# Turning the expert items' rows with a DMA transpose of two 16-bit planes

## The chip, the cores and the metric

The kernel runs on one core of one Trainium2 chip. The metric is the device time of one execution in microseconds. A core has engines that each run their own instruction stream: TensorE (PE, matrix multiply; its weight loads are listed as PEld), VectorE (DVE), ScalarE (ACT), GpSimd (POOL) and SyncE (SP). Sixteen DMA engines move data; SP, ACT and POOL issue transfers to them. SBUF is the working memory of 128 partitions, PSUM holds what TensorE writes, DRAM holds the inputs and outputs. Engines wait for one another by semaphores.

## The reference

One transformer block with adaptive layer norm, in float32, for 2 sequences of 2048 tokens and 256 features (4096 tokens in all). Six modulation vectors come from a small conditioning input.

```python
h = _layernorm(x) * (1 + ca) + sa
x = x + ga * attention(h)            # causal, 2 heads of 128, one shared k and v, rotary
h = _layernorm(x) * (1 + cb) + sb
x = x + gb * ffn(h)

# ffn: 8 experts, 256 -> 1024 -> 256, gated per token
gate = softmax(h @ Wg + bg)
thr = sigmoid(h @ Wt + bt) * 0.125
w = where(gate >= thr, gate - thr, 0); w = w / sum(w)
out = sum over e of w[e] * (gelu(h @ W1[e] + b1[e]) @ W2[e] + b2[e])
```

A token is worked on only by the experts whose weight is above zero.

## The kernel before

**Attention stage.** Work goes by tiles of 128 tokens, the two sequences in turn. For each tile the kernel loads x, normalizes it, projects q, k and v, applies the rotation, computes scores against all earlier keys in chunks of 512, takes the softmax, multiplies with v, projects, adds the residual, stores it to the output, normalizes again into `hx` (the features that the experts read), stores `hx` to the DRAM tensor `feats`, and computes the gate's logits. The order of all these steps on all engines is worked out at build time by a planner (`Plan`): each step has an engine, an assumed cost, the steps it comes after, and buffers that it takes and gives back; the planner simulates the engines and emits the steps in the order in which they would start. A changed cost can therefore change the order of every engine. The step `n_f` in `tile_steps` is the store of `hx` (issued by SP), and the step that copies the transposed `hx` for the gate comes after it. Small per-row statistics (`rstd`) are computed on POOL. At the end of each group of tiles the kernel writes the entries of expert 0's token list by indirect DMAs from POOL.

**Expert stage** (`experts`). For each expert there is a list of its tokens. The work is cut into items of up to 256 tokens (`TI`), that is two blocks of 128 (`CI`); the last item of an expert may have one block. The number of items is known only at run time, so every engine has its own loop over experts and items and they are tied together by semaphores that count up. The items are numbered through by `t`. For one item:

- POOL copies the item's token numbers into `at` (L1060) and gathers the tokens' rows of `feats` into `xr` by one indirect DMA for each block (L1018, semaphore "loaded"). `xr` is a single buffer, so POOL first waits until the previous item's rows are turned ("turned"). In the first items of each expert it also writes four pieces of the next expert's list (L1039). Then it adds an earlier item's result to the output by two indirect DMAs (L1049).
- TensorE turns the rows: features must lie on the partitions for the first product. `turn(t + 1)` (L888) makes four 128 x 128 transposes of `xr` into the PSUM tile `pT`; it stands just before the last of the eight first products of item t.
- VectorE copies `pT` to `xT` in SBUF (L963, semaphore "ready"), after the last first product of item t has read the old `xT`. `xT` is a single buffer too. After that it adds the bias to the item's result (`yb`, L986), and then waits until the earlier scatter has landed, multiplies with the gate and leaves the result in `yo`.
- TensorE multiplies with the first weights (L910, into `h`) and, two steps behind, with the second weights (L899, into `y`). In the trace a float32 matmul of one 128 x 128 weight block is two records. ScalarE applies the Gelu between the two (L937).
- SP reads each expert's list from DRAM into a sheet (L877) as soon as its last entry is written. ScalarE's queue loads the weights of experts 2 to 7.

The code touched by the change, and what calls it:

Of the kernel before, what the change touches and what calls it, by code (L numbers as in the profile page):

```python
# [11 lines left out]
F32 = mybir.dt.float32  # L12
BF16 = mybir.dt.bfloat16
I32 = mybir.dt.int32
ET = mybir.EngineType
# [4 lines left out]
P = 128  # L20
B, T, D = 2, 2048, 256
HS, NH = 128, 2
E, FF = 8, 1024
KD = D // P
# [73 lines left out]
def adaln_block_kernel(ctx, tc, x, wqkvT, woT, wgt, bgt, w1, b1T, w2, b2, cT, wmod, rope, out):  # L98
# [15 lines left out]

    nc = tc.nc
# [17 lines left out]
    feats = dram.tile([NTOK, D], F32, name="feats")  # L133
# [11 lines left out]
    for e in range(RES, E):  # L145
# [3 lines left out]
    xr = ep.tile([P, CI, D], F32, name="xr")  # L149
# [14 lines left out]
    pT = pp.tile([P, KD, TI], F32, name="pT")  # L164
    experts(
        tc, nc, lists, feats, out.rearrange("b t d -> (b t) d"), counts, ident, b1_sb, b2_bc,
        gb_bc, w1, w2, weights, xr, xT, gs, gate, part, yb, yo, sheets, at, mcur, who, to, new, place,
        entry, hs, ys, pT,
# [3 lines left out]
def attention(  # L172
# [7 lines left out]
    room = {"ps": 6, "pav": 2, "x": 9, "s": 18, "pT": 3, "hx": 4, "qT": 3, "big": 3, "xn": 3,  # L180
# [213 lines left out]
    def tile_steps(b, i, r, group, g):  # L394
# [239 lines left out]
        def hx():  # L634
# [9 lines left out]
        n_f = add(  # L644
            "SP", 0.8, lambda: nc.sync.dma_start(feats[ts(b * NT + i, P), :], st["hx"]), [n_h],
            late=2.0,
# [172 lines left out]
def experts(  # L819
    tc, nc, lists, feats, rows, counts, ident, b1_sb, b2_bc, gb_bc, w1, w2, weights, xr, xT, gs,  # L820
    gate, part, yb, yo, sheets, at, mcur, who, to, new, place, entry, hs, ys, pT,
# [40 lines left out]
    with tc.tile_critical():  # L862
        names = (
            "read", "loaded", "turned", "ready", "first", "act", "second", "taken", "parted",
            "gated", "copied", "named", "biased", "added", "waited", "indexed", "staged",
# [4 lines left out]
        with nc.Block() as block:  # L870

            @block.sync
            def _(sync):
                for e in range(E):
# [5 lines left out]

            @block.tensor
            def _(pe):
                def turn(t):

                    pe.wait_ge(sem["loaded"], t * (16 * CI) + 16 * CI)
                    for c in range(CI):
                        for k in range(KD):
                            last = pe.transpose(pT[:, k, ts(c, P)], xr[:, c, ts(k, P)], ident)  # L888
                    last.then_inc(sem["turned"], 1)

                def item(e, i, t, parts):
# [13 lines left out]
                    pe.wait_ge(sem["ready"], t + 1)  # L905
                    for f in range(NF):
                        if f == NF - 1:
                            turn(t + 1)
# [17 lines left out]
                turn(0)  # L926
# [3 lines left out]
            def _(act):  # L930
# [11 lines left out]
                def begin(e):  # L942

                    if e == 0:

                        act.wait_ge(sem["turned"], 1)
# [13 lines left out]
            def _(dve):  # L960
                def ready(t):
                    dve.wait_ge(sem["turned"], t + 1)
                    dve.tensor_copy(xT, pT).then_inc(sem["ready"], 1)  # L963
# [209 lines left out]
```

## Time and profile before

The table gives the timed runs and one profiled execution, which has a time of its own.

| what | value |
|---|---|
| runs before | median 1737.94 us of 3 (1736.16 to 1740.65) |
| the profiled execution's own time | 1731.92 us |
| its span, first to last instruction | 1729.6 us |
| mean granted TensorE clock in the span | 0.985 of full speed |
| TensorE busy | 1667.1 us, 96% of the span |
| VectorE, ScalarE, POOL busy | 669.1, 685.4, 841.4 us |
| DMA traffic | 83.61 MB, 48 GB/s over the span |

How to read it: the page cuts the span into 40 equal slices of about 43 us and gives each engine's busy share in tenths; PEclk is the granted TensorE clock in tenths. The expert stage begins about 506 us after the start. The chain that ended last follows the work back from the last instruction, each time to what released it. A timeline line gives the start and the length in microseconds, the engine, the line of the kernel, the operation, the tile written and the tiles read, the shape, and in brackets how long the engine had stood idle and who ended that. Lines of DMA issues end with the size of one and the median time from issue to landing. An engine's busy time can overlap with itself, above all TensorE's.

### The profile page before, as it was taken

Reading aid. Unit: us, or ns where it says so; the run is one execution under the profiler, and the core shown is the slowest. Engines: PE = TensorE matmul, PEld = TensorE weight load, DVE = VectorE, ACT = ScalarE, POOL = GpSimd, SP = SyncE. Lnnn points to the kernel's source line nnn. Section 1 sums busy time; section 2 is a strip of 40 time slices with the busy share of each in tenths; the row PEclk is TensorE's granted clock in tenths of the full one; section 3 lists DMA queues with packets and bytes.
Section 4 is the critical chain, followed back from the end, with each engine's and each line's share of the span. In section 5 each row is a group of like instructions: output and inputs, shape, how many; then the busy total and the mean of one; then the engine's idle time right before and its main releaser. Section 6 shows DMA issues by size and latency. Waiting matters only on the chain.

```text
span 1729.6 us, 26689 instructions
## 1 busy us (share of the span) xinstructions
PE 1667.1 (96%) x8021; PEld 1386.7 (80%) x8021; DVE 669.1 (39%) x2126; ACT 685.4 (40%) x1475; POOL 841.4 (49%) x968
## 2 busy tenths in 40 slices
PE   6899999999959999999999999999999999999996
PEld 4576666767748888888888888888888888888886
DVE  5887757566522223322222322222232222222322
ACT  1455555555513334333333333333333333333332
POOL 2331122020037757765775774666577467644433
PEclk9999999999979999999999999999999999999998
DMA  5311000000022223223223222322322222222222
GB/s 196 113 32 34 29 28 29 16 16 16 13 75 37 37 44 89 40 41 83 40 42 82 47 37 44 80 38 43 83 42 42 36 38 38 44 36 36 46 37 34
DMA packets 72489, 83.61 MB, mean 48 GB/s; under 512 B 16944, under 2 KB 63792, under 8 KB 72304
## 3 DMA queue, kind: packets, MB, share of 16 engines
q0 software_dynamic: 42784, 47.50, 17.1%
q1 hardware_dynamic: 21776, 22.86, 4.0%
q10 hardware_dynamic: 7872, 12.58, 2.2%
q8 instruction: 25, 0.41, 0.1%
q14 instruction: 32, 0.26, 0.1%
HBM read 50.38 MB, written 32.51 MB: 48 GB/s over the span
## 4 chain that ended last, share of the span: by engine, by line
PE 92%; DVE 4%; DMA 1%; issue 1%; POOL 1%; ACT 1%; POOLq 0%; SPq 0%; DVEq 0%; ACTq 0%
PE h L910 34%; PE y L899 34%; PE pav L580 7%; PE psc L498 6%; PE ptr L570 3%; PE pq L442 3%; PE pT L888 2%; PE po L614 1%; DMA list<-entry,place 1%; PE pl L661 1%; PE pr L482 1%; DVE s L509 0%; DVE x L621 0%; PE ph L652 0%; DVE hx L639 0%
## 5 line engine op out<-in xcount | busy, mean ns | idle before, releaser
L910 PE MATMUL h<-xT,w 128*128 128x256 f32 (+1 forms) x2816 | 673.5, 372 | 0.8 <-DVE xT L963 0.8
L899 PE MATMUL y<-w,g 128*128 128x256 f32 x2704 | 669.9, 379 | 0.0
L937 ACT ACTIVATE g<-h,b_sb 128x256 f32<-128x256 f32 (+1 forms) x704 | 327.6, 466 | 755.4 <-PE h L910 754.1
L910 PEld LDWEIGHTS h<-xT,w 128*128 128x128 f32 x2816 | 518.2, 191 | 67.6 <-issue 1.5
L899 PEld LDWEIGHTS y<-w,g 128*128 128x128 f32 x2704 | 510.6, 190 | 67.7
L1049 POOL DMA_INDIRECT out<-yo,who x180 | 294.6, 1636 | 119.8 <-DVE yo L998 71.8
L963 DVE COPY xT<-pT 128x512 f32<-128x512 f32 x89 | 61.6, 692 | 619.8 <-PE h L910 609.0
L1039 POOL DMA_INDIRECT list<-new,to x228 | 234.0, 1026 | 99.1 <-issue 50.3
L1018 POOL DMA_INDIRECT xr<-feats,at x178 | 179.8, 1010 | 108.2 <-POOL at L1060 74.7
L498 PE MATMUL psc<-kT,qT 128*128 128x512 f32 (+3 forms) x320 | 145.9, 542 | 1.6 <-ACT qT L487 1.1
L580 PE MATMUL pav<-pT,v 128*128 128x256 f32 x544 | 143.6, 386 | 0.8 <-ACT pT L574 0.7
L937 ACT ACT_TABLE_LOAD x88 | 112.9, 1283 | 29.1 <-issue 16.9
L525 ACT ACTIVATE s<-s,nmx 128x512 f32<-128x512 f32 (+3 forms) x160 | 104.1, 653 | 50.0 <-DVE nmx L516 49.9
L986 DVE TENSOR_TENSOR yb<-y,b_bc 128x256 f32<-128x256 f32 x169 | 64.2, 420 | 150.3 <-PE y L899 150.3
L509 DVE TENSOR_SCALAR_CACHE_REDUCE s<-psc 128x512 f32<-128x512 f32 (+3 forms) x160 | 95.4, 606 | 65.0 <-PE psc L498 44.0
L1060 POOL COPY at<-sheet 128x2 int32 (+1 forms) x88 | 44.7, 508 | 150.1 <-PE pT L888 145.9
L580 PEld LDWEIGHTS pav<-pT,v 128*128 128x128 f32 x544 | 94.8, 190 | 25.9 <-issue 14.2
L766 POOL DMA_INDIRECT list<-entry,place x32 | 34.2, 1069 | 129.4 <-DVE place L763 78.5
L574 ACT COPY pT<-ptr 128x512 f32<-128x512 f32 (+1 forms) x144 | 76.8, 563 | 47.2 <-PE pav L580 23.1
L388 POOL TENSOR_SCALAR rstdf<-mvf 128x1 f32<-128x1 f32 x32 | 9.3, 291 | 164.2 <-DVE mvf L384 68.1
L570 PEld LDWEIGHTS ptr<-ident,s 128*128 128x128 f32 x544 | 65.6, 145 | 16.4 <-ACT s L525 5.0
L977 DVE SCALAR_TENSOR_TENSOR gate<-gb_bc,mcur,part 128x256 f32<-128x256 f32 x176 | 77.5, 482 | 3.1
(133 smaller groups left out, 1145.5 us busy)
## 6 DMA issues: line engine op xcount, KB each, us to landing
w<-in_w ACTq DMA_DIRECT2D x12, 1024.0 KB, 7.4
x<-in_x SPq DMA_DIRECT2D x32, 128.0 KB, 2.1
out<-x SPq DMA_DIRECT2D x32, 128.0 KB, 1.7
feats<-hx SPq DMA_DIRECT2D x32, 128.0 KB, 1.8
w<-in_w SPq DMA_DIRECT2D x4, 1024.0 KB, 10.2
list<-new,to POOLq DMA_INDIRECT x228
out<-yo,who POOLq DMA_INDIRECT x180, 3.9
xr<-feats,at POOLq DMA_INDIRECT x178
```

What stands on the lines that cost most here:

```text
L498: nc.tensor.matmul(ps[:, :w], st["qT"][:, h, :], kT[:, ds(c * SC, w)], start=True, stop=not last)
L509: nc.vector.tensor_scalar(s[:, :w], st["sc", h, c][:, :w], 1.0, None, ALU.mult, ALU.max, accum_out=st["mx", h][:, c : c + 1],)
L525: nc.scalar.activation(s[:, :w], s[:, :w], AF.Exp, bias=st["nmx", h], accum_out=st["den"][:, h, c : c + 1],)
L570: nc.tensor.transpose(ptr[:, j, h, :], s[:, ds((c0 + j) * P % SC, P)], ident)
L580: nc.tensor.matmul(st["pav"][:, : NH * P], v[:, c0 + j, :], st["pT", c0][:, j].rearrange("p h t -> p (h t)"), start=(c0 + j == 0), stop=(c ...
L899: last = pe.matmul(ys[c], gs[f % 4][:, ts(c, P)], weights[e][1][:, f, :], start=(f == 0), stop=(f == NF - 1),)
L910: last = pe.matmul(hs[f % 4][:, :w], weights[e][0][:, k, ts(f, P)], xT[:, k, :w], start=(k == 0), stop=(k == KD - 1),)
L937: act.activation(gs[f % 4][:, :w], hs[f % 4][:, :w], AF.Gelu_apprx_tanh, bias=b1_sb[:, at : at + 1],).then_inc(sem["act"], 1)
L977: last = dve.scalar_tensor_tensor(gate[:, c, :], gb_bc[:, 1, :], mcur[:, c, 1:2], part[:, c, :], ALU.mult, ALU.add,)
L1018: pool.indirect_dma_start(out=xr[:, c, :], out_offset=None, in_=feats, in_offset=bass.IndirectOffsetOnAxis(ap=at[:, c : c + 1], axis=0),). ...
L1039: pool.indirect_dma_start(out=lists[e], out_offset=bass.IndirectOffsetOnAxis(ap=to[:, j : j + 1], axis=0), in_=new[:, j, :], in_offset=Non ...
L1049: pool.indirect_dma_start(out=rows, out_offset=bass.IndirectOffsetOnAxis(ap=who[:, c : c + 1], axis=0), in_=yo[:, c, :], in_offset=None, b ...
```

## The change

In the attention stage POOL now splits the 32-bit features of a tile into a plane of the low 16-bit halves and a plane of the high halves (`hp`), and SP stores these planes: each row of `feats` has 256 low halves and then 256 high halves, as many bytes as before. The copy for the gate now comes after the split, where it came after the store. In the expert stage the gather brings the same bytes into `xr`, seen as 16-bit elements. SP then issues one DMA transpose of `xr` (128 rows by 1024 halves) into a new SBUF tile `xp` (eight blocks of 128 x 128 halves), when the rows are loaded and VectorE has emptied `xp`; its semaphore is "planed". VectorE joins the halves of `xp` into 32-bit words of `xT` with one copy for each block. TensorE's turn, the PSUM tile `pT` and the semaphore "turned" are gone. POOL, ScalarE and VectorE wait for "planed" where they waited for "turned". SP runs a loop over experts and items of its own, and its read of the next expert's list stands in that loop after the items that write the list.

```diff
-    feats = dram.tile([NTOK, D], F32, name="feats")
+    feats = dram.tile([NTOK, 2 * D], U16, name="feats")
...
-    xr = ep.tile([P, CI, D], F32, name="xr")
+    xr = ep.tile([P, CI * 2 * D], U16, name="xr")
+    xp = ep.tile([P, CI * 2 * KD, P], U16, name="xp")
...
-        n_f = add(
-            "SP", 0.8, lambda: nc.sync.dma_start(feats[ts(b * NT + i, P), :], st["hx"]), [n_h],
-            late=2.0,
+        def halves():
+            st["hp"] = work([P, 2, D], "hp", u, U16)
+            nc.gpsimd.tensor_copy(
+                st["hp"], st["hx"].bitcast(U16).rearrange("p (d two) -> p two d", two=2)
+            )
+
+        n_f = add("POOL", 1.2, halves, [n_h], take=["hp"])
+        add(
+            "SP", 0.8,
+            lambda: nc.sync.dma_start(
+                feats[ts(b * NT + i, P), :], st["hp"].rearrange("p two d -> p (two d)")
+            ), [n_f], late=2.0, give=["hp"],
         )
...
             @block.sync
             def _(sync):
-                for e in range(E):
+                def read(e):
                     if e > 0:
                         sync.wait_ge(sem["written"], (e * NP + 1) * (16 * NW))
                     sync.dma_start(
                         sheets[e], lists[e].rearrange("(p c) f -> p c f", p=P)
                     ).then_inc(sem["read"], 16)
+                def turn(t):
+                    sync.wait_ge(sem["loaded"], t * (16 * CI) + 16 * CI)
+                    sync.sem_inc(sem["paused"], 1)
+                    sync.wait_ge(sem["ready"], t + 1)
+                    sync.sem_inc(sem["paused"], 1)
+                    sync.dma_start_transpose(xp, xr).then_inc(sem["planed"], 16)
+
+                read(0)
+                turn(0)
+                done, t0 = 1, 0
+                for e in range(E):
+                    many = items_of(sync, count(sync, e, NTOK))
+                    if e == E - 1:
+                        run(sync, many, NTOK // TI, lambda i: turn(t0 + i))
+                    else:
+                        a = count(sync, E + e, NP)
+                        run(sync, a, NP, lambda i: turn(t0 + done + i))
+                        read(e + 1)
...
+                turn(t0)
             @block.tensor
             def _(pe):
-                def turn(t):
-                    pe.wait_ge(sem["loaded"], t * (16 * CI) + 16 * CI)
-                    for c in range(CI):
-                        for k in range(KD):
-                            last = pe.transpose(pT[:, k, ts(c, P)], xr[:, c, ts(k, P)], ident)
-                    last.then_inc(sem["turned"], 1)
-
...
-                    pe.wait_ge(sem["ready"], t + 1)
+                    pe.wait_ge(sem["ready"], t + 2)
                     for f in range(NF):
-                        if f == NF - 1:
-                            turn(t + 1)
...
-                        act.wait_ge(sem["turned"], 1)
+                        act.wait_ge(sem["planed"], 16)
...
                 def ready(t):
-                    dve.wait_ge(sem["turned"], t + 1)
-                    dve.tensor_copy(xT, pT).then_inc(sem["ready"], 1)
+                    dve.wait_ge(sem["planed"], t * 16 + 16)
+                    dst = xT.bitcast(U16).rearrange(
+                        "p k (c t two) -> p c k t two", c=CI, two=2
+                    )
+                    src = xp.rearrange("p (c two k) t -> p c k t two", c=CI, two=2)
+                    for c in range(CI):
+                        last = dve.tensor_copy(dst[:, c], src[:, c])
+                    last.then_inc(sem["ready"], 1)
...
+                dve.sem_inc(sem["ready"], 1)
                 ready(0)
...
                 def item(e, i, t, also=None):
-                    wait("turned", t)
+                    wait("planed", t * 16)
...
-                wait("turned", 1)
+                wait("planed", 16)
                 scatter(0)
```

## The prediction

> **What bounds the kernel now.** I read the page's slices first, then the chain that ended last, then the timeline of one item.
>
> ```profile
> PE   6899999999959999999999999999999999999996
> PEclk9999999999979999999999999999999999999998
> PE 92%; DVE 4%; DMA 1%; issue 1%; POOL 1%; ACT 1%; POOLq 0%; SPq 0%; DVEq 0%; ACTq 0%
> ```
>
> TensorE is full from slice 12 on (from about 506 us, the expert stage) at nearly full clock, and 92% of the chain that ended last lies on it. A busy PE may overlap its own matmuls, so I go by starts. One item in the middle of the expert stage (timeline, start and length in us):
>
> ```profile
> 1003.85 1.03 PE L899 MATMUL y<-w,g 128*128 128x256 f32 x4
> ...
> 1010.76 1.03 PE L899 MATMUL y<-w,g 128*128 128x256 f32 x4
> 1011.62 0.60 PE L888 MATMUL pT<-ident,xr 128*128 128x128 f32 x4
> 1012.06 1.03 PE L910 MATMUL h<-xT,w 128*128 128x256 f32 x4
> 1012.92 2.75 PE L899 MATMUL y<-w,g 128*128 128x256 f32 x12
> 1013.21 0.69 DVE L963 COPY xT<-pT 128x512 f32<-128x512 f32 x1 [7.39 <-PE h L910]
> 1015.51 2.75 PE L910 MATMUL h<-xT,w 128*128 128x256 f32 x12
> ```
>
> A group of four matmul records takes (1010.76 - 1003.85) / 8 = 0.864 us; an item of two blocks has 16 groups, 13.82 us. The four turns take 1012.06 - 1011.62 = 0.44 from start to start, although the page gives each 273 ns (they overlap). Copies into xT stand 14.25 us apart: 13.82 + 0.43. There is no gap: TensorE sets the item, and the copy (done 1013.90, needed 1015.51) is hidden. The spacing of the 89 copies shows 88 items and one last idle turn; 7 items have one block (7.56 us).
>
> The next engine in line is POOL. Its own item where it also writes a list:
>
> ```profile
> 1013.80 0.76 POOL L1060 COPY at<-sheet 128x2 int32 x1
> 1015.41 1.02 POOL L1018 DMA_INDIRECT xr<-feats,at  x1 [0.85 <-POOL at L1060]
> ...
> 1024.27 1.61 POOL L1049 DMA_INDIRECT out<-yo,who  x1 [0.30 <-issue]
> 1026.18 1.60 POOL L1049 DMA_INDIRECT out<-yo,who  x1 [0.30 <-issue]
> 1027.19 0.80 POOL L1060 COPY at<-sheet 128x2 int32 x1
> ```
>
> From copy to copy 13.39 us with no wait for PE. In the other items (about 32) it waits up to 4.8 us for the turn, so needs about 9.4 us there. POOL is slower than nobody, but 13.4 stands close under 13.82.
>
> **The change, part by part.**
>
> *The turns leave TensorE.* Every one of the 88 items holds one turn of 0.43 us: 88 x 0.43 = -37.8 us. The chain's own share for L888, 2% of 1730 us, agrees. Nothing else was late at these points, so the next item simply starts earlier.
>
> *The DMA transpose, T, and where it lies.* SP waits until xr is loaded and the last join has emptied xp, then turns 128 x 1024 halves (256 KB) in one DMA. The join of item t ends about 1 us before item t starts, so the transpose for item t+1 starts then and is needed 13.8 - 1.2 us later: xp alone hides T up to about 11 us. Tighter is xr, also single: gather, transpose, gather. The gather's part is read at the start of the stage:
>
> ```profile
> 498.96 0.18 POOL L1060 COPY at<-sheet 128x2 int32<-128x2 int32 x1 [4.13 <-DMA sheet<-list]
> ...
> 504.08 1.12 PE L888 MATMUL pT<-ident,xr 128*128 128x128 f32 x4 [12.68 <-DMA xr<-feats,at]
> 505.24 0.69 DVE L963 COPY xT<-pT 128x512 f32<-128x512 f32 x1 [10.82 <-PE pT L888]
> 505.98 5.06 PE L910 MATMUL h<-xT,w 128*128 128x256 f32 x12 [0.78 <-DVE xT L963]
> ```
>
> From the index copy to landed data 5.1 us. The loop 5.1 + T must stay under 13.82: T up to 8.7 us costs nothing. No transpose stands in the trace. Lower end: a plain DMA.
>
> ```profile
> w<-in_w ACTq DMA_DIRECT2D x12, 1024.0 KB, 7.4
> feats<-hx SPq DMA_DIRECT2D x32, 128.0 KB, 1.8
> ```
>
> Along these two (5.6 us for 896 KB), 256 KB lands in 2.6 us. [...] so I take 3.5 us, near the rows[...]. The 16 DMA engines are 20 to 30% busy in this stage, room for 256 KB more an item. With T = 3.5 the cover is 5 us.
>
> *The join.* One copy of 0.69 us from PSUM becomes two of 512 halves each from SBUF. The nearest row is the copy sc_bc<-sc of 512 elements inside SBUF, 0.42 us; the other end is the 0.69 of now. Two make 0.84 to 1.38, with the gap about 0.9 to 1.5. The window is 1013.21 to 1015.51, 2.3 us: hidden in a whole item. In an item of one block only six records of y follow, 6 x 0.216 = 1.3 us from 1714.49, the copy began 1714.78, so 1.0 us is left: a stall of 0 to 0.5 us in 7 items, taken as +1.5 us in all. The wait for the transpose stands ahead of yb on VectorE, which PE waits for as "taken" in the next item: a late T would hit both at once.
>
> *Start of the stage, once.* From landed data to the first matmul it took 505.98 - 504.08 = 1.9 us (four turns, copy). Now T 3.5 + join 1.2 + two handovers 0.2 = 4.9: +3.0 us[...].
>
> *Waits that change owner.* POOL's gather waits for "planed" where it waited for "turned"; since the transpose runs at the start of the item before, not at its end, POOL is freed earlier and its 4.8 us waits shrink: nothing gained, it was hidden. ScalarE waits for the first transpose before it asks for expert 2's weights: 3 us later, needed twenty items on; the first Gelu behind it comes after the first matmul anyway. POOL's first scatter starts about 3 us later too; it stood at item 1's index at 512.45, over 8 us ahead of item 1. On SP the read of the next list now stands behind the transposes of the items that write it. Who waits for it are POOL and VectorE at the next expert's start; two or more items without list writes (POOL's 4.8 us waits come in runs of two or more) lie between, 27 us for a read that lands in 1.8. All these: 0.
>
> *Attention stage.* 32 times POOL splits hx into halves (512 elements) and SP stores after it. POOL's copy of 256 words took 0.63 us, the memset of 1024 took 0.94: 0.6 to 1.3 us each, 20 to 40 us in all on an engine that is 11 to 26% busy in these 500 us. The store comes about 1.3 us later; hx is held till both readers are done; the last store (486.81) then ends about 490, and the first gather is at 499.99. Behind the split on POOL stand the rstd steps, which VectorE needs. From 100 to 400 us PE is 97 to 100% busy and covers that; in the first and last 100 us (79 and 83 busy) a delay can show. The planner's costs change, so the order of the steps changes on every engine, with the same matmuls. I take 0, with -8 to +10.
>
> Sum: -37.8 + 3.0 + 1.5 = -33.3. Against the profiled execution's own 1731.92 (span 1729.6 and 2.3 around it) this is 1698.6; the runs' median 1737.94 lies 6 above it, and 1737.94 - 33.3 gives 1704.6. I say 1704.
>
> **Rivals.**
>
> A. *The transpose is the new bound* (slower). [...] It decides from 88 x (5.1 + T) = 1210, T = 8.65 us. [...] Against it: the plain rows, 3 times under that point. Chance 0.06.
>
> B. *The attention stage pays.* POOL's splits delay rstd where PE has no queue, or the new order is worse: 1.3 us on some ten tiles, +13: about 1717. For it: PE's idle time in the first and last 100 us. Against: the middle is full. Chance 0.12.
>
> C. *The join becomes a new wait.* If reading two planes alternately costs over 1.3 us a copy, the pair outlasts the 2.3 us window and each item stalls; at 1.35 us it takes back the 0.43: about 1738, no change. Against it: the 0.42 row. Chance 0.05.
>
> D. *POOL becomes the bound.* Its 13.4 us is 0.4 under the new item. [...] Chance 0.05.
>
> **Numbers.** Likeliest 0.72, at 1704, its own range 1694 to 1714. About 0.3% (5 us) is what a measurement can tell. Faster: 0.72 + B 0.12 + D 0.05 = 0.89; same: C 0.04 of its 0.05, rounded; slower: A and a rest of C, 0.07. The range leaves out A, C and the far ends: 1691 to 1720.
>
> **What the profile would show.** Right: no L888 row, matmul groups 0.864 us apart across the item's end, joins 13.82 us apart, a transpose landing in 3 to 4 us, the stage near 1175 us. Wrong: VectorE's join waiting on the transpose DMA in each item (A), PE waiting on the join (C), the join or PE waiting on gathers (D), the first expert matmul more than 10 us later than 506 (B).

## The result and the profile after

| | before | changed | difference |
|---|---|---|---|
| timed runs, median | 1737.7 us (1736.16 to 1740.65, 4 runs) | 1720.95 us (1719.86 to 1721.61, 4 runs) | ratio 0.990, 95% interval 0.988 to 0.992 |
| profiled execution | 1731.92 us | 1719.86 us | -12.1 |
| its span | 1729.6 us | 1718.0 us | -11.6 |
| granted TensorE clock | 0.985 | 0.982 | |

The change is faster by 1.0%. That is the sign that was forecast and about half of the size (1704 us, 1691 to 1720), and the time lies 1 us outside the range. The ledger of the two profiled executions, in the terms of the prediction's sum:

| part of the span | before | changed | difference | predicted |
|---|---|---|---|---|
| start to the first index copy (attention stage) | 498.96 | 504.48 | +5.5 | 0 |
| index copy to the first expert matmul | 7.02 | 9.69 | +2.7 | +3.0 |
| first to last expert matmul | 1209.97 | 1189.42 | -20.6 | -36.3 |
| last matmul to the end | 13.65 | 14.41 | +0.8 | 0 |

Two rows are off: 5.5 us in the attention stage, and 15.7 us in the expert stage. TensorE's slices, the chain that ended last and the groups of the changed kernel, from its page (busy us, mean ns, then the idle time before and who ended it):

```profile
PE   6999999999949999999999999999999999999996
PEclk9999999999979999999999999999999999999998
PE 89%; DVE 5%; DMA 2%; issue 1%; POOL 1%; ACT 1%; POOLq 0%; SPq 0%; DVEq 0%; ACTq 0%
L944 PE MATMUL h<-xT,w 128*128 128x256 f32 (+1 forms) x2816 | 675.1, 373 | 17.5 <-DVE xT L1001 17.4
L935 PE MATMUL y<-w,g 128*128 128x256 f32 x2704 | 673.5, 380 | 10.8 <-ACT g L970 8.6
L970 ACT ACTIVATE g<-h,b_sb 128x256 f32<-128x256 f32 (+1 forms) x704 | 326.3, 466 | 736.0 <-PE h L944 663.8
L1089 POOL DMA_INDIRECT out<-yo,who x180 | 295.1, 1639 | 239.1 <-DVE yo L1037 186.4
L1001 DVE COPY xT<-xp 128x512 uint16<-128x512 uint16 x178 | 72.3, 448 | 686.8 <-PE h L944 601.0
```

The row of the turns is gone, the clock is nearly the same (0.982 against 0.985, and the groups keep their 0.864 us), and TensorE still holds the chain. The first products' 17.4 us behind the join are the one wait at the start of the stage. The new thing is in the second products (L935): 10.8 us of idle time, mostly behind ScalarE's Gelu. The same row before, with POOL's scatter and index copy:

```profile
L899 PE MATMUL y<-w,g 128*128 128x256 f32 x2704 | 669.9, 379 | 0.0
L1049 POOL DMA_INDIRECT out<-yo,who x180 | 294.6, 1636 | 119.8 <-DVE yo L998 71.8
L1060 POOL COPY at<-sheet 128x2 int32 x87 | 44.6, 512 | 145.9 <-PE pT L888 145.9
```

POOL's 145.9 us of waiting for the turn are gone; it now waits 186.4 us for `yo`, at the scatter. In the order of POOL's program that is behind the gather and the list writes, so these run earlier than they did.

A two-block item in the middle of the stage went as forecast (timeline of the changed kernel):

```profile
1000.26 1.03 PE L944 MATMUL h<-xT,w 128*128 128x256 f32 x4
1001.12 2.75 PE L935 MATMUL y<-w,g 128*128 128x256 f32 x12
1001.42 0.77 DVE L1001 COPY xT<-xp 128x512 uint16<-128x512 uint16 x2 [7.72 <-issue]
1003.71 2.75 PE L944 MATMUL h<-xT,w 128*128 128x256 f32 x12
1006.30 1.03 PE L935 MATMUL y<-w,g 128*128 128x256 f32 x4
```

From the last group of first products (1000.26) to the next item's (1003.71) are 3.45 us, four groups of 0.864, with nothing between them. The two copies of the join take 0.77 us, and 1.5 us are left between their end (1002.19) and the next item. Starts of two-block items stand 13.81 us apart, where it was 14.25.

So the loss is elsewhere. Here is each one-block item by the start of its first matmul to that of the next item's:

| one-block item | 1 | 2 | 3 | 4 | 5 | 6 | sum |
|---|---|---|---|---|---|---|---|
| before | 7.47 | 7.47 | 7.54 | 7.47 | 7.60 | 7.59 | 45.1 |
| changed | 9.13 | 9.84 | 11.73 | 12.08 | 7.95 | 7.04 | 57.8 |

(The seventh ends the program.) With 0.43 us less each they should come to 42.5: the six lose 15.3 us, and three two-block items (14.26, 14.63, 15.15) another 2.6. The first of the six, with ScalarE and POOL:

```profile
655.11 1.50 PE L944 MATMUL h<-xT,w 128*128 128x128 f32 x12
656.22 0.96 POOL L1079 DMA_INDIRECT list<-new,to  x1 [0.30 <-issue]
656.71 0.37 ACT L970 ACTIVATE g<-h,b_sb 128x128 f32<-128x128 f32 x1 [2.22 <-PE h L944]
657.21 0.69 PE L935 MATMUL y<-w,g 128*128 128x256 f32 x2 [0.60 <-issue]
657.74 0.61 PE L944 MATMUL h<-xT,w 128*128 128x128 f32 x4
657.91 1.61 POOL L1089 DMA_INDIRECT out<-yo,who  x1 [0.73 <-issue]
658.90 0.37 ACT L970 ACTIVATE g<-h,b_sb 128x128 f32<-128x128 f32 x1 [1.82 <-PE h L944]
659.32 0.70 PE L935 MATMUL y<-w,g 128*128 128x256 f32 x2 [0.97 <-ACT g L970]
```

The same place before:

```profile
650.81 1.50 PE L910 MATMUL h<-xT,w 128*128 128x128 f32 x12
651.46 1.26 ACT L937 ACTIVATE g<-h,b_sb 128x128 f32<-128x128 f32 x3 [1.26 <-PE h L910]
652.15 0.60 PE L899 MATMUL y<-w,g 128*128 128x256 f32 x2
652.58 0.61 PE L910 MATMUL h<-xT,w 128*128 128x128 f32 x4
```

Before, ScalarE began 0.65 us after the item's first matmul (651.46 - 650.81); here it began 1.60 us after (656.71 - 655.11), and the three groups of first products were all finished by then. TensorE ran them at the usual pace and then stood at the second product, whose input is that Gelu. The record of TensorE's signal stands 24 ns ahead of ScalarE's start, so ScalarE was not slow: the signal came late.

I call it a late start when a Gelu begins more than 0.2 us after both its first product (by the record's end) and ScalarE's earlier work, its table load included, were done. The profiled execution of before has none; that of the changed kernel has 84, 82.7 us in all. (The expectations below count 89 with 84 us there, and 4 with 2.2 us in before. Those counts leave the table load out: the 4 of before, and 5 of the 89, are first Gelus of an item for which ScalarE was still loading its table.) In a two-block item TensorE's first products are two groups of 0.86 us ahead of the second products, and most of the late starts are hidden: 65 of them, 62.9 us in all, go with the 2.6 us that these items lose. In a one-block item the two groups are 0.43 us each, and most is paid: 19 late starts, 19.8 us in all, go with the 15.3 us.

The start of the stage answers the estimate of the transpose:

```profile
504.48 0.18 POOL L1100 COPY at<-sheet 128x2 int32<-128x2 int32 x1 [4.32 <-DMA sheet<-list]
...
509.77 1.33 SPq L901 DMA_TRANSPOSE xp<-xr  x1
...
513.30 0.82 DVE L1001 COPY xT<-xp 128x512 uint16<-128x512 uint16 x2 [13.57 <-DMA xp<-xr]
...
514.17 2.07 PE L944 MATMUL h<-xT,w 128*128 128x256 f32 x4 [17.43 <-DVE xT L1001]
```

From the issue to the join are 3.53 us (T was taken as 3.5), and from the index copy to the issue 5.3 (gather, taken as 5.1).

### The profile page after: what moved, and what is told of

It reads as the page before. It is cut to its first block, busy times and chain, and to the rows that moved or that the text cites. A ratio compares the mean times of both kernels' runs of the same rounds, so it can differ in the third digit from the quotient of the medians.

```text
span 1718.0 us, 26912 instructions
## 1 busy us (share of the span) xinstructions
PE 1635.1 (95%) x7665; PEld 1355.1 (79%) x7665; DVE 678.2 (39%) x2215; ACT 684.3 (40%) x1475; POOL 863.9 (50%) x1000
## 3 DMA queue, kind: packets, MB, share of 16 engines
q0 software_dynamic: 42784, 47.50, 17.4%
q1 hardware_dynamic: 115760, 46.21, 11.6%
## 4 chain that ended last, share of the span: by engine, by line
PE 89%; DVE 5%; DMA 2%; issue 1%; POOL 1%; ACT 1%; POOLq 0%; SPq 0%; DVEq 0%; ACTq 0%
PE h L944 34%; PE y L935 34%; PE pav L584 6%; PE psc L502 5%; PE pq L446 3%; PE ptr L574 3%; DMA list<-entry,place 1%; PE po L618 1%; DVE s L513 1%; PE pl L674 1%; PE pr L486 1%; PE ph L665 0%; DVE hx L643 0%; DVE x L625 0%; DVE t L462 0%
## 5 line engine op out<-in xcount | busy, mean ns | idle before, releaser
L944 PE MATMUL h<-xT,w 128*128 128x256 f32 (+1 forms) x2816 | 675.1, 373 | 17.5 <-DVE xT L1001 17.4
L935 PE MATMUL y<-w,g 128*128 128x256 f32 x2704 | 673.5, 380 | 10.8 <-ACT g L970 8.6
L944 PEld LDWEIGHTS h<-xT,w 128*128 128x128 f32 x2816 | 527.1, 191 | 89.0 <-DVE xT L1001 18.6
L935 PEld LDWEIGHTS y<-w,g 128*128 128x128 f32 x2704 | 511.1, 190 | 81.9 <-ACT g L970 9.3
L1089 POOL DMA_INDIRECT out<-yo,who x180 | 295.1, 1639 | 239.1 <-DVE yo L1037 186.4
L1001 DVE COPY xT<-xp 128x512 uint16<-128x512 uint16 x178 | 72.3, 448 | 686.8 <-PE h L944 601.0
L574 PE MATMUL ptr<-ident,s 128*128 128x128 f32 x544 | 76.2, 277 | 2.3 <-ACT s L529 2.1
```

Source lines behind the costliest of these rows:

```text
L574: nc.tensor.transpose(ptr[:, j, h, :], s[:, ds((c0 + j) * P % SC, P)], ident)
L935: last = pe.matmul(ys[c], gs[f % 4][:, ts(c, P)], weights[e][1][:, f, :], start=(f == 0), stop=(f == NF - 1),)
L944: last = pe.matmul(hs[f % 4][:, :w], weights[e][0][:, k, ts(f, P)], xT[:, k, :w], start=(k == 0), stop=(k == KD - 1),)
L1089: pool.indirect_dma_start(out=rows, out_offset=bass.IndirectOffsetOnAxis(ap=who[:, c : c + 1], axis=0), in_=yo[:, c, :], in_offset=None, b ...
```

## The experiments

In the diffs "-" is the changed kernel (or before, where said). The runs of before beside an experiment have a median of 1736.7 to 1738.0 us, save beside `a_hold`, `a_noadd` and `a_best2`, where they lay at 1731.0 us (1727.5 to 1731.6): those three are read against that, by their ratios, and by their profiles.

### A longer lead of TensorE

TensorE's lead is the number of groups by which its first products run ahead of its second products (`LAG`). Theory 1: the missing time is ScalarE's late starts in one-block items, and a longer lead hides them. Rival, theory 2: TensorE waits in the one-block items for something else that a lead doesn't hide.

```diff
-    LAG = 2
+    LAG = 3
```

> The changed kernel with the second products three steps behind the first instead of two (LAG 3), nothing else. Theory 1 (in items of one block TensorE's signal to ScalarE arrives up to 2.5 us late while list writes and a transpose are close together, and two steps of lead are too few to hide it): the joins around one-block items come back from 23.0-27.2 us a pair to about 21-22, the stage loses some 9 of its 16 us, about 1712. Theory 2 (the loss at the one-block items is the longer join or the wait for the transpose): the lead of ScalarE changes nothing, 1721.

Measured: 1705.85 us (1703.9 to 1708.41), ratio 0.982 (0.981 to 0.984). That is below the 1712 of theory 1 and far from the 1721 of theory 2. The expert stage takes 1175.3 us; the prediction had it near 1175. One-block items: 7.84, 7.82, 8.22, 8.25, 7.46, 7.03; all two-block items but the first 13.81. The late starts are still there, 77 of them, 64.1 us in all, but TensorE is hardly held up (2.4 us of idle time before its second products, where it was 10.8). From the one-block item (timeline, kernel with the longer lead):

```profile
658.27 0.61 PE L944 MATMUL h<-xT,w 128*128 128x128 f32 x4
659.01 0.88 ACT L970 ACTIVATE g<-h,b_sb 128x128 f32<-128x128 f32 x3 [2.60 <-PE y L935]
659.43 0.70 PE L935 MATMUL y<-w,g 128*128 128x256 f32 x2 [0.55 <-issue]
```

ScalarE stands for 2.60 us, and TensorE only for 0.55 of them. So theory 1 holds: the 0.43 us of each turn did leave TensorE, and what came back is the late starts.

### The attention stage: the split, or the order

`a_order` keeps the split of the features but plans it with the store as one step of SP, which gives the order of before. `b_order` is before, with an empty POOL step planned where the split is, which gives the new order without any split.

```diff
-        n_f = add("POOL", 1.2, halves, [n_h], take=["hp"])
-        add(
-            "SP", 0.8,
-            lambda: nc.sync.dma_start(
-                feats[ts(b * NT + i, P), :], st["hp"].rearrange("p two d -> p (two d)")
-            ), [n_f], late=2.0, give=["hp"],
-        )
+        def store():
+            halves()
+            nc.sync.dma_start(
+                feats[ts(b * NT + i, P), :], st["hp"].rearrange("p two d -> p (two d)")
+            )
+        n_f = add("SP", 0.8, store, [n_h], late=2.0)
```

> The changed kernel with the split on POOL and the store emitted as one planned step with the old cost on SP, so that the attention stage's steps stand in the order of the kernel before, with the split's work still in it. If the new order of steps cost the 5.5 us by which the stage's first index copy is later: first index copy near 499, 1715. If POOL's split itself cost it: near 504.5, 1721.

> The kernel before with the order of steps that the changed kernel has in the attention stage (an empty planned step of 1.2 on POOL ahead of the store), without the split. If the order cost the 5.5 us: 1743, first index copy near 504.5. If the split's work cost it: 1738, near 499.

Measured: `a_order` 1719.84 us (1716.96 to 1720.89), ratio 0.990 (0.988 to 0.991); `b_order` 1744.25 us (1740.84 to 1746.27), ratio 1.004 (1.002 to 1.005). The first index copy of each, from the timelines of `a_order` and of `b_order`:

```profile
499.55 0.18 POOL L1100 COPY at<-sheet 128x2 int32<-128x2 int32 x1 [4.16 <-DMA sheet<-list]
```

```profile
504.45 0.18 POOL L1061 COPY at<-sheet 128x2 int32<-128x2 int32 x1 [4.22 <-DMA sheet<-list]
```

With the split but the old order the stage ends where it did before (499.55 against 498.96). Without the split but with the new order it ends 5.5 us later (504.45), as in the changed kernel (504.48). The order costs the 5.5 us; the 32 splits, at 613 ns each, cost nothing that shows. Over all runs, the kernels of the new order have their index copy at 504.0 to 507.5 us, those of the old order at 496.7 to 502.0.

`a_order` gains nothing by it in the end: its expert stage takes 1195.3 us, 5.9 longer than that of the changed kernel, with 119 late starts, 115.1 us in all. And `b_order`, in which TensorE still turns the rows, has 26 late starts, 20.2 us in all, and one-block items of 8.4 to 9.1 us but for the last. So the late starts need neither the transposes nor a POOL freed earlier.

### A plain copy where the transpose was

```diff
-sync.dma_start_transpose(xp, xr).then_inc(sem["planed"], 16)
+sync.dma_start(xp.rearrange("p b t -> p (b t)"), xr).then_inc(sem["planed"], 16)
```

> The changed kernel with a plain DMA copy of the same 256 KB from xr to xp where the transpose was, issued at the same place of SP's queue; the turning is left out, so the experts see other numbers, and the work is the same. Theory that late starts of ScalarE come from the list writes with any DMA traffic beside them: still over 40 us of late starts, one-block items of 8 to 12 us, total 1712 to 1722. Theory that the transpose itself (its 1056 small packets, its 1.3 us of issue) makes them: late starts under 25 us, one-block items near 7.5, total near 1705. By the estimate of T, a plain copy lands 0.5 to 1 us sooner than the 3.5 us of the transpose.

Measured: 1721.54 us (one run). 109 late starts, 97.7 us in all, one-block items 9.90, 11.40, 12.40, 9.91, 7.52, 7.05. A plain DMA in the same place does much the same as the transpose. From issue to join:

```profile
511.51 0.55 SPq L901 DMA_DIRECT2D xp<-xr  x1
513.92 0.77 DVE L1001 COPY xT<-xp 128x512 uint16<-128x512 uint16 x2 [12.22 <-DMA xp<-xr]
```

2.41 us, near the 2.6 that the prediction took from the plain rows; the transpose takes 1.1 us more, 0.8 of it in this first issue (1.33 against 0.55).

### Twice the transpose

A second transpose of the same `xr` into a spare tile `xp2` runs ahead of each real one and is waited for (the lines that declare `xp2` and the semaphore are left out here).

```diff
+                    sync.dma_start_transpose(xp2, xr).then_inc(sem["extra"], 16)
+                    sync.wait_ge(sem["extra"], t * 16 + 16)
+                    sync.sem_inc(sem["paused"], 1)
                     sync.dma_start_transpose(xp, xr).then_inc(sem["planed"], 16)
```

> The changed kernel with a second transpose of the same xr into a spare tile ahead of each real one, waited for: T becomes about 7 us for every item, and 512 KB are turned for each. By the prediction T up to 8.7 us is hidden (loop of gather and transpose 5.1 + 7 = 12.1 under 13.8): two-block items stay at 13.81, only the first item starts 3.5 us later, and one-block items (7 us) may wait for their input up to 5 us each, 20 to 35 us over the seven: 1745 to 1760. By rival A's arithmetic, with a bound lower than I worked out, two-block items lengthen to over 14.5 and the total passes 1780.

Measured: 1738.70 us (1732.65 to 1746.49), ratio 1.0005 (0.9989 to 1.0021). From the first issue to the join:

```profile
509.80 1.33 SPq L902 DMA_TRANSPOSE xp<-xr  x1
513.39 1.23 SPq L905 DMA_TRANSPOSE xp<-xr  x1
516.75 0.76 DVE L1005 COPY xT<-xp 128x512 uint16<-128x512 uint16 x2 [17.02 <-DMA xp<-xr]
```

T is 6.95 us here, and the first matmul stands at 517.56, 3.4 us later than with one transpose. 70 of the 81 two-block items still take 13.81 to 13.95 us. The six one-block items sum to 65.0 us, 7.2 more than with one transpose, and the two-block items after the first lose 11 us more than there. So a T of 6.95 us is hidden in a whole item, as the prediction's cover of 8.7 us has it (no run comes up to 8.7); the one-block items, and the items next to them, have less. The total lies 6 us below my range: I had added their waits to the late starts, and perhaps the two partly fall together, which no run shows.

### Scatters ahead of the list writes

POOL adds an earlier item's result first and then writes the list.

```diff
-                    if also is not None:
-                        also()
                     add(t)
+                    if also is not None:
+                        also()
```

> The changed kernel with POOL adding the earlier item's result before it writes the list piece, so that the list writes come about 4 us later, after the transpose has landed. Theory 1 (late signals come where list writes fall into the 4 us after a transpose's issue): the late starts of ScalarE (89 over 0.2 us, 84 us in all) fall below 20, the one-block items cost 8.3 us again, about 1706. Rival (any POOL transfer near a transpose does it, so the scatters take the list writes' place): as many late starts, 1721.

Measured: 1713.3 us (1711.0 to 1715.76), ratio 0.986 (0.984 to 0.987). Late starts fall to 34, 18.5 us in all, and the one-block items to 42.6 us in sum; the total lies between the two theories. But the two-block item behind five of them takes 15.3 to 16.0 us, since the scatter, now ahead, waits for `yo` (6.73 us of idle time on POOL before the scatter at 661.95), and the next gather and transpose stand behind it:

```profile
681.12 0.83 DVE L1001 COPY xT<-xp 128x512 uint16<-128x512 uint16 x2 [8.06 <-DMA xp<-xr]
...
682.01 2.21 PE L944 MATMUL h<-xT,w 128*128 128x256 f32 x9 [1.82 <-DVE xT L1001]
```

The order of list writes and scatters bears on the late starts; in this place it brings a new wait (12.6 us over the two-block items after the first) that takes back most of what it saves.

### Scatters that don't add

```diff
                             bounds_check=NTOK - 1,
-                            compute_op=ALU.add,
```

> The changed kernel with the scatters writing rows in place of adding them to what lies in DRAM; the accumulation is left out, so the output keeps only one writer of each row, and the number of instructions is the same. 54 of the 84 us of late starts in the profile of after overlap the issue of scatters (25% of POOL's time in the stage). Theory that the adding transfer makes TensorE's signals late: late starts under 25 us, total near 1705. Theory that it does not matter what the scatter does: over 50 us, 1717 to 1722.

Measured: 1699.07 us (one run), 31.9 us below the runs of before beside it; the changed kernel lies 16.8 below its own. Late starts: none. One-block items sum to 42.5 us, as the prediction's sum wants them. Rows of the scatter and of the index copy behind it, without the add:

```profile
L1089 POOL DMA_INDIRECT out<-yo,who x180 | 190.4, 1058 | 333.1 <-DVE yo L1037 292.7 <-issue 40.4
L1099 POOL COPY at<-sheet 128x2 int32 x87 | 16.9, 194 | 9.8 <-DMA xp<-xr 8.2 <-issue 1.1
```

The copy in the changed kernel (the scatter's row stands above):

```profile
L1100 POOL COPY at<-sheet 128x2 int32 x87 | 64.2, 738 | 9.7 <-DMA xp<-xr 9.7
```

The adding scatter keeps POOL 1639 ns instead of 1058, and the two-column copy behind it takes 738 ns instead of 194. This also makes POOL's item some 1.7 us shorter, so the time alone doesn't say whether it is the adding transfer or POOL's timing. The trace says more. Call the four list writes that POOL makes in one item a set. In the changed kernel the 24 sets that begin later than 10 us into a two-block item have 2.3 us of late starts each behind them, and the 14 that begin within its first 2 us have 1.05. Without the add 21 sets still begin later than 10 us and 8 within the first 2 us, and not one late start follows. So it is not the place of the list writes alone; the place of the scatters behind them moved too, and is not separated from the add.

### List writes held back

If POOL's freedom to run ahead matters, holding its list writes should take the late starts away. `a_hold` holds them until TensorE has finished five groups of first products of the item in work (the sixth is under way, about 6 us into a two-block item); to keep the waited value positive it shifts that count by eight for every engine that reads it. `a_shift` has the shift without the hold. `a_gate` has no shift and holds the list writes until VectorE has computed an item's gate.

```diff
# a_hold (a_shift: without the last of these)
+                pe.sem_inc(sem["first"], NF)
-                        act.wait_ge(sem["first"], t * NF + (f + 1))
+                        act.wait_ge(sem["first"], t * NF + (NF + f + 1))
-                    dve.wait_ge(sem["first"], t * NF + NF)
+                    dve.wait_ge(sem["first"], t * NF + 2 * NF)
                     if also is not None:
+                        wait("first", t * NF + 5)
                         also()
# a_gate
                     if also is not None:
+                        wait("gated", t)
                         also()
```

> The changed kernel with one wait more: POOL, which the transposes let go earlier than the turns did, issues the four list writes of an item only when TensorE has finished six groups of the first product of the item in work (about 6 us into a two-block item, 3 us into a one-block one). In the profiled execution of before list writes began 3 to 11 us into the item, and ScalarE started late for 2 us in all; in that of after 22 of 57 sets begin in the last 3 us of an item and run into the next, with 2.3 us of late starts each. Theory that the earlier POOL puts list writes and the scatters behind them beside the wrong part of TensorE's item: late starts under 25 us instead of 84, one-block items near 7.5, stage near 1180, total 1706 to 1711. Theory that the phase doesn't matter: late starts over 50 us, total 1717 to 1722, or above if POOL's own period (13.4 us) no longer fits.

> The changed kernel with TensorE's count for ScalarE shifted by eight, as in the kernel that held the list writes, but nothing held. ScalarE then loads its table after the first signal of each item: two-block items 14.35 as there. Theory that phase matters: late starts come back, over 40 us, and the total is 1760 to 1775. Theory that the form of the waits did it: under 5 us of late starts, one-block items about 8.3, total 1750 to 1760.

> The changed kernel with the list writes of an item held on POOL until VectorE has computed the gate of the item in work (about 3.3 us into it); nothing else changes. Theory that the phase of the list writes and of the adding scatters behind them in TensorE's item makes the late starts: under 25 us of them instead of 84, one-block items 7.0 to 7.8, two-block ones 13.81 save those after a one-block item, total 1705 to 1711. Theory that phase doesn't matter and the form of ScalarE's waits did it in the kernel that held them before: over 50 us, total 1717 to 1723.

Measured:

| kernel | time, us | late starts | their sum, us | one-block items, sum | two-block item |
|---|---|---|---|---|---|
| changed | 1720.95 | 84 | 82.7 | 57.8 | 13.81 |
| `a_hold` | 1759.99, ratio 1.018 (1.016 to 1.019) | 0 | 0 | 50.6 | 14.35 |
| `a_shift` | 1759.78 (one run) | 55 | 52.1 | 51.3 | 14.35 |
| `a_gate` | 1798.57, ratio 1.034 (1.032 to 1.036) | 8 | 4.1 | 42.5 | 13.81 to 16.7 |

The totals of `a_hold` and `a_gate` were missed, each by a side effect of my edit, but the counts of late starts answer the question: with the shift alone they stay, with the hold they go, wholly in `a_hold` and nearly so in `a_gate`. What they cost is not read from `a_hold` and `a_shift`, whose times don't differ in favour of the hold: behind one-block items `a_hold` has five two-block items of 15.35 to 16.07 us, in which VectorE's join waits for a late transpose (TensorE stands 23.3 us behind the join in all, where it was 17.4). The shift's price is a matter of ScalarE. Its rows in the changed kernel and in `a_hold`:

```profile
L970 ACT ACT_TABLE_LOAD x88 | 112.9, 1283 | 32.2 <-issue 19.6
```

```profile
L971 ACT ACT_TABLE_LOAD x88 | 112.9, 1283 | 277.1 <-PE h L944 277.1
```

ScalarE loads its table once in every item. In the changed kernel it does so before it waits for TensorE; with the shifted count it waits first and loads then, 1.28 us on the way to the first Gelu, which lengthens every two-block item by 0.54 us. In `a_gate` the one-block items are clean, but POOL's loop closes (timeline):

```profile
728.13 0.19 POOL L1071 COPY to<-place 128x4 int32 x1 [1.49 <-DVE gate L1016]
...
731.73 0.77 DVE L1001 COPY xT<-xp 128x512 uint16<-128x512 uint16 x2 [4.07 <-DMA xp<-xr]
...
732.55 4.54 PE L944 MATMUL h<-xT,w 128*128 128x256 f32 x12 [1.98 <-DVE xT L1001]
```

The gate that I chose comes behind `yo`, which waits for the scatter before it; POOL comes late to the next gather, the transpose lands late, and TensorE waits for the join: 56 of the 80 two-block items after the first are longer, by 98 us in all.

### The kernel before with a longer lead

```diff
-    LAG = 2
+    LAG = 3
```

> The kernel before, with TensorE three groups ahead of the second matmul instead of two. In the profiled execution of before ScalarE's Gelu started late only 4 times (2.2 us in all) and its six one-block items took 7.47 to 7.60 us; yet the median of its runs lies 6 us above that execution. Theory that late starts are a property of the list writes and not of the transpose: before loses about 6 us to them in most of its runs, so a third group of lead brings 1731 to 1733. Theory that they come with the changed kernel only: 1737, no change. In both the one-block items take 7.0 to 7.8 us in the profile, and the two-block items stay at 14.25.

Measured: 1748.96 us (1748.03 to 1756.86), ratio 1.008 (1.005 to 1.011). Both theories missed. The profiled execution has 108 late starts, 89.6 us in all, where before has none, and one-block items of 10.5 to 10.7 us but for the last:

```profile
653.24 0.37 ACT L937 ACTIVATE g<-h,b_sb 128x128 f32<-128x128 f32 x1 [1.96 <-PE h L910]
...
654.21 0.61 PE L910 MATMUL h<-xT,w 128*128 128x128 f32 x4
...
655.39 0.37 ACT L937 ACTIVATE g<-h,b_sb 128x128 f32<-128x128 f32 x1 [1.79 <-PE y L899]
...
658.39 0.37 ACT L937 ACTIVATE g<-h,b_sb 128x128 f32<-128x128 f32 x1 [1.16 <-PE y L899]
658.48 0.69 DVE L963 COPY xT<-pT 128x512 f32<-128x512 f32 x1 [6.03 <-remote]
```

The longer lead, which helps the changed kernel, sets the late starts off in before: the copy into `xT` waits for the last of those signals and the next item stands behind it. The last first products of the item end at 654.82 by their record (654.21 + 0.61). ScalarE's last Gelu begins at 658.39 and VectorE's copy at 658.48, both more than 3.5 us later; it is so in five of the seven one-block items. Two engines see TensorE late at the same moment, so the delay is not one of ScalarE's own. Here POOL's list writes begin within the first 2 us of a two-block item in 36 of 56 sets; before it was 8. What a good edit is worth depends on where the other engines stand beside it.

### Joined

`a_lag3_order` is the longer lead with the old order of the attention stage. `a_best2` and `a_best3` add the hold of `a_hold` and that of `a_gate` to it.

> The changed kernel with two edits: three groups of lead instead of two in the expert stage, and the order of the attention stage as before (the split and its store planned as one step of SP). Theory that the prediction missed two separate things, +5.5 us of order and 14 to 18 us in the one-block items: index copy at 499 to 500 us, expert stage near 1175, 1705.9 - 5.5 = 1700. If the order moves things in the expert stage as well (with two groups of lead it brought nothing, 1719.8), between 1700 and 1706. Rival, that the two do not add because the late starts grow with the earlier start: 1704 to 1708.

> Three groups of lead and the order of before in the attention stage, with the held list writes. If holding them takes the late starts away, one-block items fall from 7.0 to 9.4 us to about 7.1: 1695 to 1698. If it does not, as without the hold, 1699.7, or 1702 to 1710 where POOL comes late to the gather after a one-block item.

> Three groups of lead, the order of before in the attention stage, and list writes held for the gate. If the hold takes the late starts away, one-block items are 7.03 to 7.2 and the total 1694 to 1697; if not, or if the hold makes POOL late after one-block items, 1699 to 1706.

Measured: `a_lag3_order` 1699.72 us (1698.2 to 1704.37), ratio 0.978 (0.977 to 0.980); `a_best2` 1710.47 us, ratio 0.988 (0.987 to 0.990); `a_best3` 1791.26 us, ratio 1.030 (1.028 to 1.032). The first is the fastest kernel of this study that leaves no work out, 21 us below the changed one: by the medians the 15 us of the lead and some 6 of the order add up, as expected. Its profiled execution, the slowest of the four (1704.37), shows only part of that: the expert stage takes 1176.5 us with 94 late starts, mostly hidden, and the index copy stands at 502.0, 2 us earlier than in `a_lag3`. The holds take the late starts away here too (1 and 14 left), and cost more than that is worth: in `a_best2` the one-block items take 7.84 us and the five two-block items behind them 15.4 to 15.6, in `a_best3` most two-block items take over 15 us.

## What of the prediction was right, and the step that failed

- *The turns leave TensorE: right.* 0.44 us of the two-block item (14.25 to 13.81; 88 times that is 38.7, where 0.43 gave 37.8) and 0.43 to 0.44 of the one-block items that no late start touched (7.04; 7.03 without the add). The stage near 1175 us that this implies was there in `a_lag3` (1175.3) and without the add (1171.5). "Nothing else was late at these points, so the next item simply starts earlier" is what failed, for the one-block items.
- *T, 3.5 us: right*, 3.53 from issue to join. It was my estimate: the rows of plain transfers gave 2.6, and how far above them a transpose would lie was not shown by the trace of before (a plain copy in the same place took 2.41, so the transpose is 1.1 us longer). A T above 8.65, on which rival A rests, was not shown either. Rival A is out; with T at 6.95 us whole items still kept their length.
- *The join: right in the two-block item* (0.77 us for the pair, a little under the 0.84 to 1.38 that I had bounded it by, hidden). *In the one-block item* I took +1.5 us in all for a join that would be late. It was not: 7.03 to 7.04 us where nothing else was late. Rival C is out.
- *The start of the stage: right*, +2.7 for +3.0.
- *Waits that change owner, "All these: 0": wrong; this is the step that failed. The handovers in the expert stage gave back 17.9 us where the sum had 0.* I saw that POOL would be freed earlier and wrote "nothing gained, it was hidden". I asked only whether POOL would wait less, and not what it would do with the time. Its gather and list writes moved forward against TensorE's items: of 56 sets of list writes, 31 began 4 to 10 us into a two-block item before and 7 after; later than 10 us it was 1 before and 24 after. The late starts grew from none to 82.7 us, and the one-block items, where the lead is half as long, paid 15.3 us, the three two-block items 2.6. Shown: the one-block items lose it by late starts (they come back to 42.5 or 42.6 us in sum in `a_swap`, `a_noadd` and `a_gate`, and most of the way with the longer lead of `a_lag3`); the late starts vanish without the adding of the scatters (`a_noadd`), and don't need the transposes (`a_plain`, `b_order`); holding the list writes on POOL takes them away (`a_hold` against `a_shift`, and nearly so `a_gate`); the order of list writes and scatters matters (`a_swap`). Argued, not shown: that it was POOL's earlier release by which this change brought them.
- *Attention stage, 0 with -8 to +10: the sign open, the size in its range.* It cost +5.5 us. Of the two reasons named under rival B it was the planner's new order, not splits that delay `rstd`.
- *Rival D, POOL as the bound: not seen.* That anything would lengthen POOL's 13.4 us was not shown by the trace of before, and two-block items with list writes keep 13.81 us.

The sum with the measured terms: -38.7 for the turns, +17.9 given back in the expert stage, +2.7 at its start, +5.5 in the attention stage and +0.8 at the end come to -11.8; the spans differ by -11.6. The 5.5 us of the order lay inside its stated range; what the expert stage gave back is half of the forecast gain.

What stays open: why the signal is late. In the trace the records of the matmuls overlap (a group of four is 1.03 us long, and the next starts 0.86 us after it), so it can't tell a matmul that ended late from a signal that took long; the matmuls behind it start on time. Position in the item alone is not the cause: in `a_gate` 47 of 56 sets begin later than 10 us into an item, with 0.02 us of late starts each, where those of the changed kernel have 2.3. And that the earlier POOL is how the change brought the late starts about is argued from the shift of the list writes and from the holds; no run puts POOL back exactly where the turns had held it. `b_order` and `b_lag3`, in which the turns still hold POOL, have late starts too (20.2 and 89.6 us), so an earlier POOL is not the only way to them. It is open too why the timed runs of before mostly lie 6 us above its profiled execution (the seven beside `a_hold` do not: their median is 1731.0); one-block items like those of `b_order` would do it, but the test that I made for it (`b_lag3`) set off something else.

## What to carry to other kernels

When an edit removes a wait from an engine off the critical path, say where in the bottleneck's cycle that engine's next work will then stand, and check the shortest cycle as well as the usual one: the lead that hides a late handover in a long item was half as long in a short one (two groups of 0.43 us against two of 0.86). A step that a planner places costs its order too (5.5 us here), and an empty step in the old kernel separates that cost from the step's own work in one run. Test a repair in the company it will run in: one more group of lead gained 15 us in the changed kernel and lost 12 in the old one.

## What was not expected of the hardware

- TensorE's signals reached ScalarE late in the changed kernel (0.98 us on average over the 84 late starts, 3.8 at most), while TensorE's own records kept their pace until it needed the Gelu. Each of the 84 came within 9 us after POOL began a set of list writes, and there was none when the scatters behind them did not add. In `b_lag3` VectorE saw TensorE's signal late together with ScalarE (658.48 and 658.39 us).
- An adding scatter of 128 rows kept POOL 1639 ns and a plain one 1058; the transfers on POOL's queue took 42,784 packets for 47.50 MB with the add and 25,504 for the same bytes without it. A POOL copy of two columns behind adding scatters took 738 ns on average in the changed kernel (512 in before, where it first waited for the turn), 194 behind plain ones.
- The issue of one transpose of 256 KB held SP's queue 1.24 us in the median (0.80 to 1.55). At the start of the stage it was 1.33 us, and that of a plain copy of the same bytes 0.55 us there (`a_plain`).
- Shifting the value of one semaphore count moved ScalarE's table load of 1.28 us from ahead of its wait to behind it, and lengthened each two-block item by 0.54 us.
